# Toeplitz loads begun by SyncE alone, the first tile of a projection made ahead, and another order of pieces in the attention

## The chip, the cores and the metric

The kernel runs on one core of a Trainium2 chip. A core has five engines that each work through their own list of instructions in order: TensorE (PE, matrix multiplication, with its weight loads shown as PEld), VectorE (DVE), ScalarE (ACT), GpSimd (POOL) and SyncE (SP). Data moves between the chip's memory and the on-chip SBUF by DMA. A DMA is begun by an instruction on one of the engines (here SP, ACT or POOL), and that instruction stands in the engine's list like any other. Matrix products land in PSUM and are moved from there by DVE or ACT.

The metric is the device time of one execution in microseconds (us); the median of several runs is compared. A profile of one execution comes beside it.

## What is computed

The input is 8 images of 56 x 56 pixels with 192 channels, in float32. Four layers follow each other, each of the form x + f(group_norm(x)) with 32 groups. The first two are alike and take most of the time; cut to what matters:

```python
# layers 0 and 1, x normalized, 192 -> 576 channels
p = silu(x @ p_w.T + p_b)
q = silu(x @ q_w.T + q_b)
v = silu(x @ v_w.T + v_b)
qv = q * v
o1 = toeplitz(qv along w, a1)     # one 56-tap two-sided filter per channel
o2 = toeplitz(qv along h, a2)
out = (p * (o1 + o2)) @ o_w.T + o_b
```

Layer 2 is a 7 x 7 depthwise convolution, a layer norm and a two-layer MLP with GELU. Layer 3 is attention with 6 heads in shifted windows of 7 x 7:

```python
q, k, v = x @ Wq, x @ Wk, x @ Wv          # 6 heads of 32, windows of 49 tokens
attn = softmax(q @ k.T * sqrt(32) + bias + masks)
out = (attn @ v) @ Wfc + bfc
```

## The kernel before

**Layers 0 and 1.** The images are handled in two halves of four, named by j0 = 0 and 2. For each layer and half there are three parts, each a Python generator that yields now and then:

- `tno_qv` (Q): normalizes x, multiplies by the weights of q and v, applies Silu and the product, and stores qv to memory. It runs over groups of 256 tokens. A group's x comes by one DMA on SP (L222, buffer pool `t6`, three buffers) two groups ahead; it is normalized on ACT (`normalize`, L228, six instructions per group). A unit is up to 128 tokens by 512 columns: 16 matmuls for each 256 columns (L245), a bias addition on DVE (L254), Silu on ACT (L264), the product on DVE (L267) into a buffer of the pool `t4`, and a store by a DMA on SP (L270).
- `tno_toeplitz` (TZ): 9 blocks of 64 channels by two directions (d = 0 along w, d = 1 along h) make 18 steps; each layer and half has such a run, which makes 72 steps in all. A step n loads its matrices with two DMAs (`matrices`, L331, buffers `tm0` and `tm1` in turn) and its qv with two DMAs (L317, along w) or one (L320, along h) into one of two buffers `q`; both are asked for two steps ahead, when the last `along` of step n has been given out, because that frees the buffers. Then come eight `along` (32 matmuls, L343, and a copy to `ot` on ACT, L350) and eight `turned` (seven transposes on PE, L360, and a copy or an addition into `s` on DVE, L363 and L366). The sum is stored by POOL (L376).
- `tno_out` (O): for tiles of 224 tokens, loads x (L112, in a helper) and the sum s = o1 + o2 (L436) by DMAs on SP, normalizes x on DVE (`normalize`, three tensor_scalar, L442, into a `t4` buffer), multiplies by the gate's weights (L460, L475), takes Silu on ACT (L504, into two more `t4` buffers, and L521), multiplies s by the gate (L531), and multiplies that by the output weights for the tile before (L470, L492), adds x and stores.

`weave` runs a *lane*, a list of Q and O generators, and takes pieces of one Toeplitz generator in between, in proportion. When 90% of a generator's planned time is done it begins the next one (`then`) by calling it at each yield until it returns a value other than None. The lanes are: Q(0,0); Q(0,2) with TZ(0,0); O(0,0) and Q(1,0) with TZ(0,2); O(0,2) and Q(1,2) with TZ(1,0); O(1,0) with TZ(1,2); O(1,2) with layer 2. In the profile Q(0,2) lies from about 456 to 1090 us, the next three lanes end near 2080, 3150 and 3800 us.

**Layer 3** (`attention`). Sixteen units of half an image, each in three groups g of windows. In each group there are four slots, in which pieces of other units may be given to PE: after the scores of i = 0, after those of i = 1, after the transposes of the previous group's weights (`turned`, L1223), and between the two halves of the product with v (`weighted`, L1245). A table says which kind goes into each slot: 0 is the next unit's projection (`project`: Wq, Wk, Wv; 64 matmuls of L1155 in a piece, with copies L1168 on ACT and L1170 on DVE), 1 is the previous unit's output (`out`: matmuls L1271 in two pieces, drained from PSUM by DVE, L1282).

```python
order = ((0, 0, 0, 0), (0, 1, 1, 0), (0, 0, 0, 0))
```

**What sets the order.** The framework's scheduler decides each engine's order of instructions from a planned time of each; engines then run in order. PSUM is a pool of four buffers of two banks (`bank2`), so PE waits when the four before it have not been emptied.

Of the kernel before, what the change touches and what calls it, by code (L numbers as in the profile page):

```python
# [19 lines left out]
B, H, W, C = 8, 56, 56, 192  # L20
# [16 lines left out]
class Net:  # L37
# [266 lines left out]
    def tno_toeplitz(self, j0, tables, qv, o):  # L304

        nc, p = self.nc, self.tz
        PR = H // 2

        def load(n):
            blk, d = divmod(n, 2)
            q = p.tile([128, H, 128], F32, name="q", bufs=2)
            if d == 0:
                for half, eng in ((0, nc.sync), (1, nc.scalar)):
                    of = qv[2 * blk + half, :T].rearrange("(h w) e -> w h e", w=W)
                    eng.dma_start(q[64 * half : 64 * half + W], of)  # L317
            else:
                of = qv[2 * blk : 2 * blk + 2].rearrange("n (h w) e -> (n h) (w e)", w=W)
                nc.scalar.dma_start(q.rearrange("p i e -> p (i e)"), of)  # L320
            return q

        def matrices(n):

            blk, d = divmod(n, 2)
            tab = tables[d]
            for half in range(2):
                at = tab.offset + (blk * DC + 32 * half) * 112
                src = bass.AP(tab.tensor, at, [[1, H], [112, 32], [1, H]])
                to = self.tms[n % 2][64 * half : 64 * half + H, : 32 * H]  # L330
                nc.scalar.dma_start(to.rearrange("p (c w) -> p c w", w=H), src)  # L331

        def along(n, q, ot, g):


            tm = self.tms[n % 2]
            pt = self.bank2()
            for j in range(4):
                c = 4 * g + j
                for s in range(2):  # L340
                    for r in range(2):
                        rows = slice(64 * r, 64 * r + 56)
                        nc.tensor.matmul(  # L343
                            pt[64 * s : 64 * s + 64, r, j * 112 : (j + 1) * 112],
                            tm[rows, c * H : c * H + 64],
                            q[rows, PR * s : PR * s + PR, 4 * c : 4 * c + 4],
                            start=True,
                            stop=True,
                        )
            nc.scalar.copy(  # L350
                view(ot, 4 * g, [[112 * 32, 2], [32, 112], [1, 4]]),
                view(pt, 0, [[512, 2], [1, 112], [112, 4]]),
            )

        def turned(d, ot, s, r, i0, n):

            pz = self.bank2().rearrange("p k (i q) -> p (k i) q", q=128)
            for i in range(n):
                at = (r * PR + i0 + i) * 128
                nc.tensor.transpose(pz[:, i, :120], ot[:120, at : at + 128], self.ident[:120, :120])  # L360
            if d == 0:
                to = view(s, r * T + i0 * W + 55, [[W, n], [PR * W, 2], [-1, W]])
                nc.vector.tensor_copy(to, view(pz, 0, [[128, n], [64, 2], [1, 56]]))  # L363
            else:
                to = view(s, r * T + 55 * W + i0, [[-W, H], [PR, 2], [1, n]])
                nc.vector.tensor_add(to, to, view(pz, 0, [[1, 56], [64, 2], [128, n]]))  # L366

        def store(blk, s, half):
            for b in range(4):
                part, row = divmod(blk * DC + 32 * half, 128)  # L370
                if part < 4:
                    part += b // 2 * 4
                else:
                    part, row = 8, row + b // 2 * 64
                to = o[j0 + b % 2, part, row : row + 32, :]
                nc.gpsimd.dma_start(to, s[32 * b : 32 * b + 32, half, :])  # L376

        NS = 2 * (D1 // DC)
        loaded = []
        for n in range(2):  # L380
            loaded.append(load(n))
            matrices(n)
        yield 8.0

        late = []
        for n in range(NS):
            blk, d = divmod(n, 2)
            q = loaded.pop(0)
            ot = p.tile([128, 2 * PR * 128], F32, name="ot", bufs=1)
            if d == 0:  # L390
                s = p.tile([128, 2, T], F32, name="s", bufs=1)
            for g in range(8):
                along(n, q, ot, g)
                if g % 4 == 3:
                    if g == 7 and n + 2 < NS:
                        loaded.append(load(n + 2))
                        matrices(n + 2)
                    yield 3.2
                    for f in late:
                        store(*f)  # L400
                    late = []
            for u in range(8):
                turned(d, ot, s, u // 4, u % 4 * 7, 7)
                if u % 4 == 3:
                    yield 3.2
                    for f in late:
                        store(*f)
                    late = [(blk, s, u // 4)] if d == 1 else []
        for f in late:
            store(*f)  # L410

    def tno_out(self, L, j0, xs, gn, o, ys, gn_next):

        nc, p, inp = self.nc, self.tp, self.inp
        N = 224
# [16 lines left out]
        def load_s(j, t):  # L434
            s = p.tile([128, 9, N], F32, name="t8")
            nc.sync.dma_start(s, o[j, :, :, t * N : (t + 1) * N].rearrange("k p t -> p k t"))  # L436
            return s
# [104 lines left out]
        before = None  # L542
        x2 = load_x(*tiles[0])
        s = load_s(*tiles[0])
        yield 0.0
        xn = normalize(j0, x2[:, :, :N])
        done = None
        for n, (j, t) in enumerate(tiles):
            self.norm_part()
# [65 lines left out]
    def tno_layers(self, x0, x1, x2, gn, last):  # L615
# [3 lines left out]
        LS = ("L0", "L1")  # L619
# [9 lines left out]
        with ExitStack() as ctx, ExitStack() as wqp:  # L629
            self.wqp = wqp.enter_context(tc.tile_pool(name="wqp", bufs=1, side="right"))  # L630
            self.tp = ctx.enter_context(tc.tile_pool(name="tp", bufs=3))
            Q = lambda i, j0: self.tno_qv(LS[i], j0, x[i], gn[i], qvs[j0])
            O = lambda i, j0: self.tno_out(LS[i], j0, x[i], gn[i], o[i], x[i + 1], gn[i + 1])
            TZ = lambda i, j0: self.tno_toeplitz(j0, tables[i], qvs[j0], o[i])
            QT, OT, TZT = 25 * 2.25 * 5.3, 28 * 10.7, 8 + 72 * 3.2

            with tc.tile_pool(name="tab", bufs=2) as tab:
                self.input_stats(x0, gn[0], 0, tab)
                self.decay_tables("L0", tab, tables[0])
                first = Q(0, 0)  # L640
                for n in range(20):
                    next(first)
                self.input_stats(x0, gn[0], 2, tab)
                none = tab.tile([112, 512], F32, name="none", bufs=1)
                nc.gpsimd.memset(none, 0.0)
                for qv in qvs.values():
                    to = qv[:, T:].rearrange("n (p k) e -> p n (k e)", p=112)
                    nc.gpsimd.dma_start(to, view(none, 0, [[0, D1 // 32], [1, 512]]))
                self.decay_tables("L1", tab, tables[1])
                lanes = [[(first, QT)], [(Q(0, 2), QT)], [(O(0, 0), OT), (Q(1, 0), QT)]]  # L650
                lanes += [[(O(0, 2), OT), (Q(1, 2), QT)], [(O(1, 0), OT)], [(O(1, 2), OT)]]
                self.weave(lanes[0], after=lanes[1][0][0])
            with tc.tile_pool(name="tz", bufs=1) as self.tz:
                self.tms = []
                for i in range(2):
                    tm = self.tz.tile([120, 32 * H + 8], F32, name=f"tm{i}")
                    nc.gpsimd.memset(tm, 0.0)
                    self.tms.append(tm)
                for n, tz in enumerate((TZ(0, 0), TZ(0, 2), TZ(1, 0), TZ(1, 2))):
                    self.weave(lanes[n + 1], tz, lanes[n + 2][0][0], TZT)  # L660
                    if n == 2:
                        wqp.close()
            self.weave(lanes[5], **last())
# [320 lines left out]
    def attention(self, L, xs, gn3, gnd, ys, vd):  # L984
# [14 lines left out]
        if True:  # L999
# [321 lines left out]
            late = None  # L1321


            order = ((0, 0, 0, 0), (0, 1, 1, 0), (0, 0, 0, 0))
            for n in range(len(units) + 1):
                if n < len(units):
                    (b, hh), (v, qf, kf) = units[n], now
# [3 lines left out]
                for g in range(NG):  # L1331
# [1 line left out]
                        outs = out(*units[n - 1], *raws.pop(n - 1), oj)  # L1333

                    def give(at):
                        if order[g][at] and outs is not None:
                            step(outs)
                        elif not order[g][at] and gen is not None:
                            return step(gen)
                        return now  # L1340

                    es = []
                    for i in range(2):
# [218 lines left out]
```

## Time and profile before

| what | us |
|---|---|
| median of three runs | 6429.96 (6421.82 to 6434.29) |
| the profiled execution | 6428.51 |
| its span | 6426.7 (1.8 outside of it) |
| mean granted clock of TensorE | 0.943 |

By stretch, with PE's busy time, PE's clock (1.00 is full speed), the DMA engines' busy share and what they moved:

| stretch, us | work | PE busy | PEclk | DMA share | GB/s |
|---|---|---|---|---|---|
| 456 to 1090 | Q(0,2), TZ(0,0) | 558.06 | 0.93 | 0.84 | 223 |
| 1090 to 1650 | O(0,0), TZ(0,2) | 492.59 | 0.92 | 0.75 | 202 |
| 1650 to 2080 | Q(1,0), TZ(0,2) | 399.97 | 0.98 | 0.69 | 188 |
| 2080 to 2700 | O(0,2), TZ(1,0) | 552.58 | 0.92 | 0.71 | 196 |
| 2700 to 3150 | Q(1,2), TZ(1,0) | 413.03 | 0.96 | 0.66 | 181 |
| 3150 to 3800 | O(1,0), TZ(1,2) | 553.98 | 0.90 | 0.84 | 220 |
| 3800 to 4400 | O(1,2), layer 2 | 556.69 | 0.95 | 0.60 | 207 |
| 4400 to 5440 | layer 2 | 1022.88 | 0.99 | 0.37 | 117 |
| 5440 to 6427 | attention | 863.51 | 0.91 | 0.38 | 78 |

How to read lines of the profile: L343 is line 343 of the kernel. `out<-in` gives the buffers by their names in the program. A bracket at the end of a timeline line, as in `[2.85 <-DVE ra L1282]`, is the time for which the engine stood idle before, and what ended it. `ACTq` and `SPq` are the queues of DMA instructions on these engines: the length of such a line is the time in which the engine dealt with beginning the DMA, not that of the data's way. The page's last part lists DMAs by size:

```profile
q<-qv ACTq DMA_DIRECT2D x36, 3584.0 KB
...
tm<-L_tab ACTq DMA_DIRECT2D x144, 392.0 KB
q<-qv SPq DMA_DIRECT2D x36, 1568.0 KB
q<-qv ACTq DMA_DIRECT2D x36, 1568.0 KB
```

So the Toeplitz part begins its loads of q and of the matrices on both queues: 36 on SP and 36 + 36 + 144 on ACT.

### The profile page before, as it was taken

How to read it: one execution, taken by the hardware profiler on the slowest of the kernel's cores; microseconds unless marked ns; L12 is line 12 of the kernel's file. 1: busy time of each engine (PE TensorE's matmuls, PEld its weight loads, DVE VectorE, ACT ScalarE, POOL GpSimd, SP SyncE). 2: the span in 40 equal slices, each digit the busy share in tenths (PEclk: the TensorE clock that was granted, in tenths of full speed). 3: DMA queues.
4: the chain of work that ended last, by engine and by line, in shares of the span. 5: the costliest groups of instructions: out<-in, count | busy, mean ns of one | idle time of the engine just before them, and what ended most of it. 6: DMA issues, size and time to landing. Idle time of an engine off the chain costs nothing.

```text
span 6426.7 us, 151998 instructions
## 1 busy us (share of the span) xinstructions
PE 5783.7 (90%) x68832; PEld 4566.2 (71%) x68832; DVE 2860.1 (45%) x4858; ACT 2148.7 (33%) x2736; POOL 635.6 (10%) x829
## 2 busy tenths in 40 slices
PE   5998898899999899898888889998999999898897
PEld 3777787787777778777777778885666444666665
DVE  6554555344555444455434343324212322555555
ACT  2444343232444222344232323224323333333332
POOL 0000000000000000000000010000000100333332
PEclk9998999999999999999988999999999999999998
DMA  7448887777675677675698865664444322443432
GB/s 247 116 145 217 225 253 182 209 201 214 182 200 163 178 214 204 186 213 161 174 228 213 256 198 193 218 237 127 166 152 152 93 61 59 73 87 85 90 82 56
DMA packets 1240518, 1078.47 MB, mean 168 GB/s; under 512 B 452704, under 2 KB 1186912, under 8 KB 1224448
## 3 DMA queue, kind: packets, MB, share of 16 engines
q1 hardware_dynamic: 825768, 620.03, 34.9%
q10 hardware_dynamic: 378648, 247.74, 15.1%
q0 software_dynamic: 35456, 200.98, 9.8%
q8 instruction: 541, 8.86, 0.6%
q14 instruction: 105, 0.86, 0.0%
HBM read 712.50 MB, written 356.12 MB: 166 GB/s over the span
## 4 chain that ended last, share of the span: by engine, by line
PE 70%; DVE 10%; DMA 8%; ACT 5%; issue 3%; ACTq 2%; POOL 1%; SPq 1%; DVEq 0%; POOLq 0%
PE bank L245 16%; PE bank L360 7%; PE bank L881 6%; PE bank L460 5%; PE bank L470 5%; PE bank L343 5%; PE bank L742 5%; PE bank L961 4%; PE bank L1155 2%; PE bank L975 2%; DMA qv<-t 2%; PE bank L475 2%; PE bank L492 2%; ACT ot L350 2%; DVE t L254 2%
## 5 line engine op out<-in xcount | busy, mean ns | idle before, releaser
L245 PE MATMUL bank<-wq,t 64*128 64x256 f32 (+5 forms) x8000 | 1319.9, 372 | 66.9 <-ACT ot L350 49.1
L245 PEld LDWEIGHTS bank<-wq,t 64*128 64x128 f32 (+3 forms) x8000 | 1041.0, 189 | 319.1 <-issue 104.9
L264 ACT ACTIVATE t<-t 128x2048 f32<-128x2048 f32 (+1 forms) x300 | 439.9, 1482 | 960.8 <-DVE t L254 872.4
L254 DVE TENSOR_TENSOR t<-bank,wq 128x1024 f32<-128x1024 f32 (+2 forms) x500 | 540.2, 1113 | 477.1 <-PE bank L245 476.2
L360 PE MATMUL bank<-ident,ot 120*128 120x120 f32 x4032 | 549.0, 300 | 162.7 <-ACT ot L350 64.7
L360 PEld LDWEIGHTS bank<-ident,ot 120*128 120x128 f32 x4032 | 494.6, 160 | 222.7 <-DVE s L363 78.1
L504 ACT ACTIVATE t<-bank,wo 128x448 f32<-128x448 f32 x448 | 247.5, 635 | 1065.3 <-PE bank L475 795.8
L343 PE MATMUL bank<-q,tm 56*64 56x112 f32 x18432 | 522.6, 266 | 70.8 <-issue 32.8
L531 DVE TENSOR_TENSOR t<-t,t 128x896 f32<-128x896 f32 x224 | 241.4, 1090 | 752.9 <-ACT t L504 752.0
L343 PEld LDWEIGHTS bank<-q,tm 56*64 56x64 f32 x18432 | 482.1, 138 | 105.9 <-issue 57.1
L350 ACT COPY ot<-bank 128x896 f32<-128x896 f32 x576 | 481.6, 916 | 158.2 <-PE bank L343 157.4
L460 PE MATMUL bank<-t,wo 128*128 128x224 f32 x1792 | 405.1, 382 | 85.8 <-ACT t L504 46.4
L460 PEld LDWEIGHTS bank<-t,wo 128*128 128x128 f32 x1792 | 358.0, 207 | 106.5 <-ACT t L504 58.2
L267 DVE TENSOR_TENSOR t<-t 128x1024 f32<-128x1024 f32 (+1 forms) x300 | 280.5, 955 | 317.0 <-ACT t L264 253.8
L881 PE MATMUL bank<-z,w 128*128 128x448 f32 (+1 forms) x1344 | 413.2, 555 | 2.0 <-ACT h L890 2.0
L470 PE MATMUL bank<-t,wo 128*128 128x224 f32 x1792 | 367.2, 359 | 7.8 <-DVE t L531 4.9
L470 PEld LDWEIGHTS bank<-t,wo 128*128 128x128 f32 x1792 | 346.1, 194 | 11.9 <-DVE t L531 5.3
L363 DVE COPY s<-bank 128x784 f32<-128x784 f32 x288 | 267.7, 970 | 152.7 <-PE bank L360 122.9
L742 PEld LDWEIGHTS bank<-xt,cm 113*112 113x112 f32 x3072 | 309.2, 178 | 36.1 <-issue 31.7
L881 PEld LDWEIGHTS bank<-z,w 128*128 128x128 f32 (+1 forms) x1344 | 182.2, 189 | 205.5 <-issue 196.8
L376 POOL DMA_DIRECT2D L_sum<-s x288 | 141.0, 496 | 1821.5 <-DVE s L366 1816.0
L742 PE MATMUL bank<-xt,cm 113*112 113x108 f32 (+2 forms) x3072 | 317.4, 263 | 3.5 <-ACT h L890 2.4
(141 smaller groups left out, 6814.8 us busy)
## 6 DMA issues: line engine op xcount, KB each, us to landing
q<-qv ACTq DMA_DIRECT2D x36, 3584.0 KB
L_sum<-s POOLq DMA_DIRECT2D x288, 392.0 KB, 7.2
t<-L_sum SPq DMA_DIRECT2D x112, 1008.0 KB
qv<-t SPq DMA_DIRECT2D x192, 512.0 KB
cm<-in_L_cm SPq DMA_DIRECT2D x96, 896.0 KB
tm<-L_tab ACTq DMA_DIRECT2D x144, 392.0 KB
q<-qv SPq DMA_DIRECT2D x36, 1568.0 KB
q<-qv ACTq DMA_DIRECT2D x36, 1568.0 KB
```

The source lines that it names most:

```text
L245: nc.tensor.matmul(pp[:m, b, 256 * j : 256 * j + k], x[rows, j, 2 if part else b, s : s + m], w[rows, part, c0 + c : c0 + c + k],  start=p ...
L254: nc.vector.tensor_add(z[:m, c : c + k, :], view(pp[:m], 0, [[1, k], [256, 4]]), view(bias[:m], c0 + c, [[1, k], [0, 4]]),)
L264: nc.scalar.activation(z[:m, :n, :], z[:m, :n, :], AF.Silu)
L267: nc.vector.tensor_mul(prod[:m, :k], half[:, :, 0], half[:, :, 1])
L343: nc.tensor.matmul(pt[64 * s : 64 * s + 64, r, j * 112 : (j + 1) * 112], tm[rows, c * H : c * H + 64], q[rows, PR * s : PR * s + PR, 4 * c ...
L350: nc.scalar.copy(view(ot, 4 * g, [[112 * 32, 2], [32, 112], [1, 4]]), view(pt, 0, [[512, 2], [1, 112], [112, 4]]),)
L360: nc.tensor.transpose(pz[:, i, :120], ot[:120, at : at + 128], self.ident[:120, :120])
L363: nc.vector.tensor_copy(to, view(pz, 0, [[128, n], [64, 2], [1, 56]]))
L460: mm(gs[c // 2][:, b, c % 2 * 256 : c % 2 * 256 + N], pw[:, 0, 128 * c : 128 * c + 128], xn[:, b], start=c % 2 == 0, stop=False,)
L470: mm(P[:, b, :N], ow[:, c, 0:128], g[:, 4 * b + c], start=c == 0, stop=False)
L742: nc.tensor.matmul(pc[:, 128 * e + 4 * m0 : 128 * e + 4 * m1], cm[:113, e, k, :], xt[:, m0 - 1 + k : m1 - 1 + k, c + e, :], start=n == 0 a ...
L881: nc.tensor.matmul(phs[c][:, s, :TT], w0[rows, part, at : at + 128], z[rows, Z[2 if part else s], :], start=part == flip, stop=part != flip,)
```

## The change

It has three parts. First, the loads of q and of the matrices in `tno_toeplitz` are all begun by SP; before, ACT began one half of the pairs of L317 and all of L320 and L331. Second, `tno_out` takes a flag `early`: with it, the generator yields None after its first loads, so that `weave` calls it once more and the first tile's normalize is given out before the generator's own turn. It is set for all but O(1, 2). Third, the table of the attention's slots holds lists of kinds. In group 1 the second slot now takes an output piece and then a projection piece, the third slot an output piece, and the fourth none; before, the projection piece stood in the fourth.

```diff
-                for half, eng in ((0, nc.sync), (1, nc.scalar)):
+                for half in range(2):
                     of = qv[2 * blk + half, :T].rearrange("(h w) e -> w h e", w=W)
-                    eng.dma_start(q[64 * half : 64 * half + W], of)
+                    nc.sync.dma_start(q[64 * half : 64 * half + W], of)
             else:
...
-                nc.scalar.dma_start(q.rearrange("p i e -> p (i e)"), of)
+                nc.sync.dma_start(q.rearrange("p i e -> p (i e)"), of)
...
-                nc.scalar.dma_start(to.rearrange("p (c w) -> p c w", w=H), src)
+                nc.sync.dma_start(to.rearrange("p (c w) -> p c w", w=H), src)
...
-    def tno_out(self, L, j0, xs, gn, o, ys, gn_next):
+    def tno_out(self, L, j0, xs, gn, o, ys, gn_next, early):
...
         s = load_s(*tiles[0])
+        if early:
+            yield None
+            xn = normalize(j0, x2[:, :, :N])
         yield 0.0
-        xn = normalize(j0, x2[:, :, :N])
+        if not early:
+            xn = normalize(j0, x2[:, :, :N])
...
-            O = lambda i, j0: self.tno_out(LS[i], j0, x[i], gn[i], o[i], x[i + 1], gn[i + 1])
+            O = lambda i, j0, early=True: self.tno_out(LS[i], j0, x[i], gn[i], o[i], x[i + 1], gn[i + 1], early)
...
-                lanes += [[(O(0, 2), OT), (Q(1, 2), QT)], [(O(1, 0), OT)], [(O(1, 2), OT)]]
+                lanes += [[(O(0, 2), OT), (Q(1, 2), QT)], [(O(1, 0), OT)], [(O(1, 2, False), OT)]]
...
-            order = ((0, 0, 0, 0), (0, 1, 1, 0), (0, 0, 0, 0))
+            order = (((0,), (0,), (0,), (0,)), ((0,), (1, 0), (1,), ()), ((0,), (0,), (0,), (0,)))
...
-                        if order[g][at] and outs is not None:
-                            step(outs)
-                        elif not order[g][at] and gen is not None:
-                            return step(gen)
-                        return now
+                        got = now
+                        for kind in order[g][at]:
+                            if kind and outs is not None:
+                                step(outs)
+                            elif not kind and gen is not None:
+                                got = step(gen)
+                        return got
```

## The prediction

> **What bounds the kernel now.** I read the page's first and fourth part, then the waits of PE and of ACT, then busy times and clock by stretch, then the timeline around the largest stalls.
>
> ```profile
> PE 5783.7 (90%) x68832; PEld 4566.2 (71%) x68832; DVE 2860.1 (45%) x4858; ACT 2148.7 (33%) x2736; POOL 635.6 (10%) x829
> ...
> PE 70%; DVE 10%; DMA 8%; ACT 5%; issue 3%; ACTq 2%; POOL 1%; SPq 1%; DVEq 0%; POOLq 0%
> ```
> PE is the bound: it is idle for 6426.7 − 5783.7 = 643 us. The change adds and removes no PE work, so it can gain only from this idle time and from matmuls that run at half clock. The waits of PE that it touches (total us, times, longest):
>
> ```profile
> PE bank L360 <- ACT ot L350: 64.7, 27, 6.3
> PE bank L360 <- DVE s L363: 62.6, 53, 5.0
> PE bank L1271 <- DVE ra L1282: 47.0, 30, 3.6
> PE bank L460 <- ACT t L504: 46.4, 5, 17.5
> PE bank L460 <- DVE t L442: 32.6, 12, 8.1
> ```
> The second is untouched; it shows that not all waits of a Toeplitz step go. What ACT waits for shows who ends the fourth, and how late x tiles already come:
>
> ```profile
> ACT t L504 <- DMA qv<-t: 79.9, 3, 29.1
> ACT t L228 <- DMA t<-in_x: 66.1, 16, 13.9
> ```
> [...] In three consecutive stretches of an attention unit (PE, PEld, DVE, ACT, POOL busy, then PEclk, DMA share, GB/s) it falls after PE's idle and rises again:
>
> ```profile
> 5962.60:5971.90 9.30, 6.45 (x76) 4.26 (x72) 6.07 (x13) 2.48 (x4) 4.55 (x3) 1.00 0.44 69
> 5971.90:5978.70 6.80, 6.17 (x152) 4.58 (x152) 3.53 (x11) 0.00 (x0) 0.00 (x0) 0.50 0.34 120
> 5978.70:5985.50 6.80, 6.80 (x268) 5.07 (x264) 3.79 (x6) 2.25 (x2) 0.05 (x1) 1.00 0.62 163
> ```
> So a gap of 2.85 us costs up to 6.80 × 0.5 = 3.4 us more.
>
> [...] one L331 issue held ACT's queue for 16.6 us (longest of 144; median 0.34). [...]
>
> **Part 1, Toeplitz loads from ACT to SP.** 36 L317, 36 L320 and 144 L331 leave ACT (216 issues, 1295 to 1511 on SP). The recorded lengths of these issues add up to some 600 us of ACT's queue between 456 and 3800 us, but ACT is busy 33% and most of it lies beside idle ACT. What counts is what stands behind them. At a step's end an L331 waits until PE has read the old matrix, and the last copies L350 stand behind it:
>
> ```profile
> 1251.04 1.70 ACT L350 COPY ot<-bank 128x896 f32<-128x896 f32 x2
> 1252.40 0.31 ACTq L331 DMA_DIRECT2D tm<-L_tab  x1
> 1252.63 0.93 ACT L350 COPY ot<-bank 128x896 f32<-128x896 f32 x1
> 1252.78 1.97 ACTq L320 DMA_DIRECT2D q<-qv  x1
> 1253.42 0.94 ACT L350 COPY ot<-bank 128x896 f32<-128x896 f32 x1
> ```
> PE's L360 after it is idle 2.07 us, against about 1.1 where no issue stands between. There are 12 such ends of 2.0 to 2.1 us in the three lanes with tno_out: 12 × 0.9 = 11 us, and the six of the first two lanes are each followed by 3.4 us at half clock (1.7 us lost): up to 10, I take 8. In the lane from 456 to 1090 seven ends wait 3.2 to 6.3 us. In the new order of ACT's instructions the 2048-wide Silu L264 (1.9 us) stands ahead of the last copies there as now, so the five of 3.58 stay, and only 5.13 and 6.27 come down to that: 4 us. At each lane's start L320 (3.6 MB) is begun on ACT beside the qv stores, L267 waits for a store (11.1 us at 484), and PE for L254: 8.09 us at 479, and 3.80, 3.38 and 6.55 us in the two later stretches in which tno_qv runs beside the Toeplitz. In the new SP order this load comes 25 us later in the first lane: half of these 22, 10 us. The long issues leave little on PE (0.90 and 0.39 us after those of 15.3 and 16.6): 3. Sum 36, taken as **−35** (−15 to −60).
>
> Its price lies on SP. [...] from packet times in this trace (0.027 us for 512 B, 0.041 for 896 B) I estimate 14 to 16 us of full-rate transfer per step. Behind them stand L222 (next x of tno_qv), L270 (qv stores), L436 and L112 (s and x of tno_out). An SP issue that waits for its matrix or q buffer holds all of these. L222 has 7 to 19 us from issue to use where I followed it (611.5 to 625.6, 664.7 to 671.6, 721.8 to 729.7), L436 15 or more. Beside the times at which before issued them, the new order moves most neighbours by 1 to 5 us, and L222 behind stores by 8 to 11 in about 11 of 29 cases. With 28 x groups each 3 us later, ACT waits 84 us more in L228; of the 66 us it waits now in the lane from 456, PE shows about 19, so 84 × 19/66 = 24: **+25** (0 to +60).
>
> **Part 2, first tile of a projection ahead.** It acts where the last product of tno_qv meets the first tile of tno_out: 1110, 2117 and 3138 us (the fourth, O(1, 2), keeps the old way).
>
> ```profile
> 1111.01 0.32 ACTq L317 DMA_DIRECT2D q<-qv  x1
> 1111.43 1.91 ACT L264 ACTIVATE t<-t 64x2048 f32<-64x2048 f32 x1 [5.04 <-DMA q<-qv]
> ...
> 1142.99 2.21 ACT L504 ACTIVATE t<-bank,wo 128x448 f32<-128x448 f32 x4 [29.14 <-DMA qv<-t]
> ```
> These are ACT's; PE's, in the same place:
>
> ```profile
> 1115.38 6.30 PE L460 MATMUL bank<-t,wo 128*128 128x224 f32 x16 [5.44 <-DVE t L442]
> ...
> 1124.94 1.78 PE L460 MATMUL bank<-t,wo 128*128 128x224 f32 x8 [0.50 <-DVE t L442]
> ...
> 1144.20 3.35 PE L460 MATMUL bank<-t,wo 128*128 128x224 f32 x8 [17.48 <-ACT t L504]
> ```
> The L317 on ACT waits for stores to land and holds a Silu 5.0 us; with it L267 and then L442 are late, and PE loses 5.4. The last two stores go out at 1119 to 1122 behind the loads of q, x and weights and land at 1143; L504 waits for their t4 buffers, and PE loses 17.5. In the new order L442 stands about ten DVE instructions earlier, the L317 is on SP, and only its first half (1.6 MB, about 5.8 us) stands before the last two stores, which should land near 1120, about when PE has done the 10.5 us of gate matmuls it can do. Three times both (17.48 + 13.55 + 14.06, 3 × 5.4 and 3 × 0.5) are 62.8 us, and half clock over the matmuls that follow some 4 each: 75. Late next are the stores themselves (0 to 3 us) and the t4 buffer that the early tile holds during the last products (0 to 5): I take off 5 each. **−60** (−25 to −75). Three tensor_scalar and the loads of a tile move earlier and are none more; q(1), the L320 that now comes later, is first read some 90 us on.
>
> **Part 3, attention.** In 14 units the projection piece (64 matmuls, 1.54 + 0.96 us at L1155) moves from between the halves of L1245 to ahead of the transposes L1223. PE now finishes L1223 and waits 2.85 and then 0.63 us for PSUM that DVE empties:
>
> ```profile
> 5969.99 2.65 DVE L1282 SCALAR_TENSOR_TENSOR ra<-bank,bfc,ra 128x371 f32<-128x371 f32 x8
> ```
> The drains start where they did, after the row sum that waits for the exponentials. With the piece in front, 2.4 us of the gap are filled, but L1223 and the second L1271 then wait for the same buffers: 1.2 + 0.4 + 0.65 = 2.25 us against 3.5. So 1.25 × 14 = 17 us; if no gap is long enough to drop the clock, 14 × 3.4 = 48 more. With half of that, **−40** (0 to −65); below nothing only if L1245 then waits for L1233, now hidden by the second L1271 (4.8 us).
>
> **Sum.** −60 − 35 + 25 − 40 = −110: 6428.5 becomes 6318.5. The profiled run lies 1.5 us below the median of 6429.96, which gives 6320.
>
> **Rivals.** (1) *The cover of the DMA holds the gain* (DMA share is 0.84 in the lane from 456 and 0.84 from 3150). Late stores still end the three transitions, and the clock falls in attention anyway: −25 − 15 + 25 − 18 = −33, 6397. [...] Against: the stall of 17.5 us has one store order behind it, and that order changes. (2) *x tiles come late, slower*: in the three lanes with tno_qv beside the Toeplitz, L222 stands behind a whole step's block. The gains are 135 us; over 28 groups this decides at 4.8 us of PE time lost per group. At 6 it is 168 − 135 = +33, about 6463. For it: 66 us of such waits already, and slack as low as 7 us. Against: mostly 1 to 5 us of shift in the order. (3) *Part 3 does nothing*, its gap only moving: 6360. This lies in the forecast's own case.
>
> **How the numbers follow.** The forecast's case, 6260 to 6365, gets 0.62; rival 1 (to 6417) 0.20; no change 0.05; rival 2 0.13. A measurement here can tell about 0.2%, 13 us, from no change. Faster 0.82, same 0.05, slower 0.13. The range 6265 to 6415 leaves out rival 2, no change and the far end of the sum.
>
> **What would show it.** Right: L460's two waits fall from 46.4 + 32.6 to 25 or less (the fourth lane's stay); L360 on L350 from 64.7 to about 50; L1271 on L1282 falls with new small waits at L1223; PEclk rises in the transitions. Wrong: ACT's L228 waits for x well above 145 (66.1 + 78.9), PE idle behind them, SP issues of 10 us and more with L222 behind; attention as long as before; L504 still waiting 20 us for stores.

## The result and the profile after

The changed kernel takes 6267.16 us (median of four runs, 6264.8 to 6269.64) against 6427.83 us for the kernel before (median of four runs, 6421.82 to 6434.29): the ratio is 0.975, with a 95% interval of 0.9733 to 0.9767, or 160.7 us less. The forecast was 6320, 110 us less. The profiled span is 6263.0 us. Line numbers after L545 have moved by 4 and, from L1341 on, by 6: L1275 is the old L1271, L1286 the old L1282, L1227 the old L1223.

The first and fourth part of the page of the changed kernel:

```profile
PE 5694.4 (91%) x68832; PEld 4501.3 (72%) x68832; DVE 2853.2 (46%) x4858; ACT 2148.3 (34%) x2736; POOL 637.6 (10%) x829
...
PE 66%; DVE 10%; DMA 9%; ACT 6%; issue 5%; SPq 2%; POOL 1%; POOLq 0%; ACTq 0%; DVEq 0%
```

PE has done the same 68832 matmuls in 89.3 us less busy time (5783.7 − 5694.4), and the mean granted clock is 0.958 after 0.943 (at 0.50 for 525 us of the span, after 733 us): more of the matmuls ran at full clock. PE is idle 74 us less (643 to 568.6). What PE waited for, in the rows that answer to those of before (total us, times, longest):

```profile
PE bank L245 <- ACT ot L350: 100.5, 44, 11.2
...
PE bank L360 <- ACT ot L350: 56.4, 25, 5.5
...
PE bank L460 <- DVE t L442: 24.6, 5, 8.0
...
PE bank L1227 <- DVE ra L1286: 20.9, 14, 1.9
PE bank L1249 <- DVE et L1237: 18.4, 15, 2.1
...
PE bank L360 <- DVE s L363: 5.6, 2, 2.8
...
PE bank L1275 <- DVE ra L1286: 5.6, 14, 1.3
```

Three things are to be seen. The row that the prediction called untouched, L360 behind L363, is nearly gone: 62.6 to 5.6 us. L460 behind L504 (46.4) has gone altogether. And one row has doubled: L245 behind L350 is 100.5 us, and before it was

```profile
PE bank L245 <- ACT ot L350: 49.1, 37, 2.9
```

To see where the time went, the span is cut at the first matmul of each part (times from the traces, in us; the columns to the right are differences from before):

| stretch | before | after | loads alone (e1) | q alone (e4) | matrices alone (e10) | rotation (e9) |
|---|---|---|---|---|---|---|
| Q(0,2) with TZ(0,0) | 638.1 | +33.7 | +34.1 | +38.5 | +52.1 | +3.4 |
| O(0,0) with TZ(0,2) | 537.0 | −62.8 | −65.0 | −57.2 | −44.1 | −13.9 |
| Q(1,0) with TZ(0,2) | 470.2 | +10.0 | +16.2 | +30.1 | +34.0 | +11.2 |
| O(0,2) with TZ(1,0) | 543.7 | −70.1 | −73.6 | −63.0 | −49.2 | −25.2 |
| Q(1,2) with TZ(1,0) | 476.8 | +0.4 | +9.8 | +29.3 | +38.7 | +8.4 |
| O(1,0) with TZ(1,2) | 709.0 | −34.6 | −39.9 | −40.5 | −38.0 | −21.4 |
| attention from its first scores | 943.8 | −37.9 | +4.1 | −4.5 | −13.5 | −10.9 |

The rest of the span moves by 9 us or less. Each column is one execution, and stretches scatter: in e2 and e3 below, whose Toeplitz loads are those of before, a stretch of layers 0 and 1 differs from before by up to 13.3 us, and the attention takes 930 to 948 us with the old order in all these runs, 899 to 907 with the new one. The execution of e9 is its fastest, 24 us below its median. In these traces the gain is −167.5 in the three stretches with `tno_out` and −37.9 in the attention; +44.1 is given back where `tno_qv` runs beside the Toeplitz.

The same Toeplitz step shows most of it. PE before, at the step from 1207.5:

```profile
1207.55 0.94 PE L360 MATMUL bank<-ident,ot 120*128 120x120 f32 x7
1209.65 0.94 PE L360 MATMUL bank<-ident,ot 120*128 120x120 f32 x7 [1.17 <-DVE s L363]
1211.66 0.94 PE L360 MATMUL bank<-ident,ot 120*128 120x120 f32 x7 [1.07 <-DVE s L363]
1213.66 1.66 PE L360 MATMUL bank<-ident,ot 120*128 120x120 f32 x7 [1.07 <-DVE s L363]
1216.39 1.66 PE L360 MATMUL bank<-ident,ot 120*128 120x120 f32 x7 [1.07 <-DVE s L363]
1219.12 4.46 PE L360 MATMUL bank<-ident,ot 120*128 120x120 f32 x21 [1.07 <-DVE s L363]
```

and after, at the same step:

```profile
1222.64 5.96 PE L360 MATMUL bank<-ident,ot 120*128 120x120 f32 x56
```

Before, the eight groups of seven transposes run in turn with the copies of DVE, and from the fourth group on at half clock (1.66 instead of 0.94 us, PEclk 0.50 from 1213.7 to 1223.9): 1207.55 to 1223.4, or 15.8 us. After, all 56 run through in 6.0. The reason can be read from the two programs as built, in the PSUM buffers (named by their first bank) that these eight groups were given:

```
before: 2 2 2 2 2 2 4 2
after:  4 6 2 0 4 6 2 0
```

A buffer that holds the group just before is refilled only after DVE has emptied it: the five waits of 1.07 to 1.17 us above. Before, 72 of all 576 groups take their neighbour's buffer, in sixteen steps, all in stretches with `tno_out`; after, none does. PE's order of work is almost the same in both. The section on the kernel before was too simple here: PE does not wait until four earlier buffers are empty, but for the one buffer that the plan gave it, and the plan does not take the four in turn.

### The profile page after: what moved, and what is told of

It reads as the page before. It is cut to its first block, busy times and chain, and to the rows that moved or that the text cites. A ratio compares the mean times of both kernels' runs of the same rounds, so it can differ in the third digit from the quotient of the medians.

```text
span 6263.0 us, 151859 instructions
## 1 busy us (share of the span) xinstructions
PE 5694.4 (91%) x68832; PEld 4501.3 (72%) x68832; DVE 2853.2 (46%) x4858; ACT 2148.3 (34%) x2736; POOL 637.6 (10%) x829
## 3 DMA queue, kind: packets, MB, share of 16 engines
q1 hardware_dynamic: 1204416, 867.77, 53.7%
## 4 chain that ended last, share of the span: by engine, by line
PE 66%; DVE 10%; DMA 9%; ACT 6%; issue 5%; SPq 2%; POOL 1%; POOLq 0%; ACTq 0%; DVEq 0%
PE bank L245 15%; PE bank L360 6%; PE bank L885 6%; PE bank L746 5%; PE bank L460 5%; PE bank L470 5%; PE bank L965 4%; PE bank L343 4%; PE bank L979 2%; DVE t L254 2%; PE bank L475 2%; DMA t<-x 2%; ACT ot L350 2%; ACT t L264 2%; PE bank L492 2%
## 5 line engine op out<-in xcount | busy, mean ns | idle before, releaser
L245 PE MATMUL bank<-wq,t 64*128 64x256 f32 (+5 forms) x8000 | 1330.5, 374 | 115.8 <-ACT ot L350 100.5
L245 PEld LDWEIGHTS bank<-wq,t 64*128 64x128 f32 (+3 forms) x8000 | 1050.4, 191 | 369.0 <-ACT ot L350 111.3
L343 PE MATMUL bank<-q,tm 56*64 56x112 f32 x18432 | 533.9, 268 | 110.2 <-issue 54.5
L343 PEld LDWEIGHTS bank<-q,tm 56*64 56x64 f32 x18432 | 488.5, 139 | 150.3 <-issue 86.2
L360 PE MATMUL bank<-ident,ot 120*128 120x120 f32 x4032 | 482.7, 282 | 69.1 <-ACT ot L350 56.4
L504 ACT ACTIVATE t<-bank,wo 128x448 f32<-128x448 f32 x448 | 248.1, 636 | 832.4 <-PE bank L475 808.4
L350 ACT COPY ot<-bank 128x896 f32<-128x896 f32 x576 | 482.1, 915 | 138.8 <-PE bank L343 138.5
L360 PEld LDWEIGHTS bank<-ident,ot 120*128 120x128 f32 x4032 | 452.3, 150 | 107.7 <-ACT ot L350 62.1
L267 DVE TENSOR_TENSOR t<-t 128x1024 f32<-128x1024 f32 (+1 forms) x300 | 283.5, 956 | 387.5 <-ACT t L264 332.4
L460 PE MATMUL bank<-t,wo 128*128 128x224 f32 x1792 | 387.7, 371 | 25.2 <-DVE t L442 24.6
L460 PEld LDWEIGHTS bank<-t,wo 128*128 128x128 f32 x1792 | 346.0, 199 | 40.5 <-DVE t L442 16.8
L470 PE MATMUL bank<-t,wo 128*128 128x224 f32 x1792 | 362.7, 356 | 13.1 <-DVE t L531 10.7
L470 PEld LDWEIGHTS bank<-t,wo 128*128 128x128 f32 x1792 | 342.1, 192 | 16.0 <-DVE t L531 6.1
L363 DVE COPY s<-bank 128x784 f32<-128x784 f32 x288 | 260.4, 965 | 85.0 <-PE bank L360 45.1
```

The source lines that it names most:

```text
L245: nc.tensor.matmul(pp[:m, b, 256 * j : 256 * j + k], x[rows, j, 2 if part else b, s : s + m], w[rows, part, c0 + c : c0 + c + k],  start=p ...
L267: nc.vector.tensor_mul(prod[:m, :k], half[:, :, 0], half[:, :, 1])
L343: nc.tensor.matmul(pt[64 * s : 64 * s + 64, r, j * 112 : (j + 1) * 112], tm[rows, c * H : c * H + 64], q[rows, PR * s : PR * s + PR, 4 * c ...
L350: nc.scalar.copy(view(ot, 4 * g, [[112 * 32, 2], [32, 112], [1, 4]]), view(pt, 0, [[512, 2], [1, 112], [112, 4]]),)
L460: mm(gs[c // 2][:, b, c % 2 * 256 : c % 2 * 256 + N], pw[:, 0, 128 * c : 128 * c + 128], xn[:, b], start=c % 2 == 0, stop=False,)
L470: mm(P[:, b, :N], ow[:, c, 0:128], g[:, 4 * b + c], start=c == 0, stop=False)
```

## The experiments

After the result, and before the first of these runs, two theories stood against each other. A: the loads' part gains through those PSUM buffers. B, the prediction's: it gains because ACT's queue is no longer held by issues of DMAs. Ratios are against the kernel before, run beside each on the same chip.

**e1, the first part alone.** The three edits of `tno_toeplitz` and nothing else.

> The Toeplitz loads on SP alone, without the early tile and without the other order in attention. Theory A (PSUM buffers: in the program before, 72 of 576 groups of transposes L360 get the very PSUM buffer of the group just before them and so run in turn with DVE; with the loads off ACT none do): the 62.6 us of L360 behind L363 and most of the 24.9 behind L366 go, with some 30 us of half clock, and the later x tiles cost about 45: near 6350 us. Theory B (the prediction's: ACT's queue is held by the issues): -35 + 25, near 6418, and L360's waits for DVE stay above 50 us.

Measured: 6313.31 us, ratio 0.9806 (0.9778 to 0.9834), 119.0 us less than the 6432.3 beside it. L360's wait for L363 is 6.9 us. Theory A's sign and rows come true, and the gain is larger than its number: the three stretches with `tno_out` lose 178.5 us, which includes the transitions. Both marks of B are missed, 6418 us and waits for DVE above 50 us.

**e2, the second part alone.** The edits of `tno_out`, its flag and the lanes, as in the change.

> The early first tile alone. If the late L442 and the t4 buffers are the cause of the transitions' stalls (62.8 us): about -45, near 6385. If the loads' place on the queues causes them, as the order of the last two stores behind q loads suggests: less than -15, near 6415. L360's waits for DVE stay at 62.6 in both.

Measured: 6434.97 us, ratio 1.0005 (0.9993 to 1.0017), as the second of the two forecasts has it. The stall has only moved: PE's waits at the three transitions were 62.8 us before and are 75.0 here (28.02 + 23.47 + 23.53). PE of this run at the first transition, and under it the DVE instruction that it waits for:

```profile
1132.68 3.29 PE L460 MATMUL bank<-t,wo 128*128 128x224 f32 x16
...
1166.77 5.91 PE L460 MATMUL bank<-t,wo 128*128 128x224 f32 x16 [28.02 <-DVE t L442]
```

```profile
1166.22 1.01 DVE L442 TENSOR_SCALAR t<-t,gn 128x224 f32<-128x224 f32 x3 [26.56 <-DMA qv<-t]
```

The first tile's matmuls now start without a wait, but the second tile's normalize needs a `t4` buffer, and that is held by a qv store that has not landed. What was late were the stores; L442 and L504 only stood in line for them.

**e3, the third part alone.** The table of slots and the function `give` that reads it, as in the change.

> The attention's order alone. Prediction: -40, near 6388. The stretch from the first scores to the end was 943.8 us before and is 905.9 after: if the gain is the order's own, it is -38 here too; if it were owed to something earlier (DMA, weights), it would be under -20.

Measured: 6392.56 us, ratio 0.9939 (0.9919 to 0.9959), 39.7 us less. The attention's stretch is 900.1 us here, 43.7 shorter. The gain is the order's own.

**e4, only the q loads to SP.** The edits of L317 and L320; L331 stays on ACT.

> Only the loads of q (L317, L320) go to SP; the 144 matrix loads L331 stay on ACT with their waits and holds of up to 16 us. Theory A: 1 of 576 transposes' groups keeps its neighbour's buffer, so nearly the whole gain in the stretches with tno_out is there: within 25 us of e1. Theory B: the L331 ahead of the last copies still hold ACT, so half of e1's gain or more is missing.

Measured: 6364.82 us, ratio 0.9889 (0.9863 to 0.9914). This is 51.5 us above e1, more than the 25 that theory A allowed, and less than the half of e1's 119.0 us that theory B wanted missing. The table shows where they are. In the stretches with `tno_out` the gain is all but whole (−160.7 against −178.5), with 144 L331 still on ACT and L360's wait for L363 at 7.6 us. The difference lies in the stretches with `tno_qv` (+97.9 against +60.1). The total alone would have misled.

**e5, the buffers shared again in the changed kernel.** `turned` gets the tile of the group before it in the sixteen steps concerned.

```diff
-            pz = self.bank2().rearrange("p k (i q) -> p (k i) q", q=128)
+            if not same:
+                shared[0] = self.bank2()
+            pz = shared[0].rearrange("p k (i q) -> p (k i) q", q=128)
...
-                turned(d, ot, s, u // 4, u % 4 * 7, 7)
+                turned(d, ot, s, u // 4, u % 4 * 7, 7, 1 <= u <= one.get(n, 0))
```

> The changed kernel, but the groups of transposes that shared a PSUM buffer with their neighbour in the kernel before (72 of 576, in 16 steps of runs 1 to 3) are made to share it again; the loads stay on SP. Theory A: L360's waits for L363 and L366 come back to about 85 us, with some 30 us of half clock: 100 us or more above the changed kernel, near 6370. Theory B: the waits have another cause (ACT held by its DMA issues, and DVE behind it): under 30 us, below 6300.

Measured: 6292.84 us, ratio 0.9793 (0.9763 to 0.9822). The time lies where theory B put it, but it tests neither theory: the built program shows that the scheduler saw the sharing and put other matmuls between the groups, so none directly follows its neighbour in the same buffer any more, and the wait for DVE is 9.3 us. The state before could not be made again in this way.

**e6, the change without its second part.**

> The change without its early tile: loads on SP and the attention's order. e1 and e3 together gave -159 of the whole's -161. If the early tile is worth nothing: 6260 to 6280. If it has the -45 that the expectation of e2 gave it, beside the loads: 6310.

Measured: 6277.54 us, ratio 0.9769 (0.9741 to 0.9798), which overlaps the whole change's 0.9733 to 0.9767. The early tile is worth nothing that the times can tell, with the loads on SP (here) or without (e2). The traces do show a little beside the loads on SP: at the three transitions PE waits 23.0 us for L442 in this run, and 15.6 in the whole change.

**e7 and e8, x of `tno_qv` begun by another engine.** `nc.sync` of L222 becomes `nc.scalar` (e7) or `nc.gpsimd` (e8) in the changed kernel.

> The changed kernel with the x loads of tno_qv (L222) begun by ACT. If these loads are late [...], their ACT waits (209 us) fall below 80 and the three stretches with tno_qv get back most of their +44: near 6230. If DMA as a whole is the limit there: within 10 us of 6267. A loss would show as ACT holding its own copies behind a waiting x load.

> The same loads begun by POOL, which is busy 10%: as e7, near 6230, but without holding ACT; POOL's stores L376 would stand behind a waiting x load, which costs little since they have slack.

Measured: e7 6329.24 us, ratio 0.9845 (0.9818 to 0.9872); e8 6243.59 us, ratio 0.9718 (0.9688 to 0.9748). In neither do ACT's waits for x fall: they are 305 us in e7 and 232 in e8, against 209 in the changed kernel and 145 before. With x begun by ACT these waits are 96 us longer than in the changed kernel, and the kernel loses. On POOL it is 34 us faster than e6 (6277.54), which ran on the same chip but lacks the early tile; against the whole change (0.9733 to 0.9767) the intervals overlap. The stretches with `tno_qv` give back 28.7 us where the change gives 44.1, but 39.2 in e11, which begins the loads in the same way, so it is not shown where the gain lies. It does not come from the waits that were to fall below 80: x that no longer stands on SP's queue is not earlier.

**e9, the kernel before with a fixed rotation of PSUM.** All loads are where they were.

```diff
-        ps = ctx.enter_context(tc.tile_pool(name="ps", bufs=4, space=PSUM))
-        self.bank2 = lambda: ps.tile([128, 2, 512], F32, name="bank2")
+        ps = ctx.enter_context(tc.tile_pool(name="ps", bufs=1, space=PSUM))
+        self.turn = 0
+
+        def bank2():
+            self.turn = (self.turn + 1) % 4
+            return ps.tile([128, 2, 512], F32, name=f"bank2{'abcd'[self.turn]}")
+
+        self.bank2 = bank2
```

> The kernel before, all its loads where they were (ACT and SP), but its four PSUM buffers are handed out in a fixed rotation instead of by planned time; 12 instead of 72 of the 576 groups of transposes then take their neighbour's buffer. Theory A: L360's waits for L363 and L366 fall from 87 to below 30 us, and the time by 50 to 100: 6330 to 6380. Theory B (ACT held by its issues): within 20 us of before, and L360's waits for DVE above 50.

Measured: 6408.45 us, ratio 0.9966 (0.9953 to 0.9979): 22 us less, not half of the least that A expected, and just beyond B's 20. Lines are 6 higher here: L366 is the transposes, L369 and L372 what DVE does with them, L510 the gate's Silu on ACT, L337 the loads of the matrices. What ended PE's waits at the transposes (us, times):

```profile
  ACT ot L356: 63.1, 27
  ACT t L510: 60.9, 9
  DVE s L369: 22.0, 15
  DVE s L372: 10.9, 10
```

The waits for DVE are down from 87.5 (62.6 behind L363 and 24.9 behind L366 before) to 32.9 us, a little more than A said and less than B's 50. In their place stand 60.9 us behind Silus of the gate, which are late on ACT and hold PSUM; before, this wait was 1.5 us. The trace shows why they are late. One of the nine, first on ACT and then on PE:

```profile
1289.86 15.01 ACTq L337 DMA_DIRECT2D tm<-L_tab  x1
1304.97 1.16 ACT L510 ACTIVATE t<-bank2b,wo 128x448 f32<-128x448 f32 x2 [18.90 <-issue]
```

```profile
1306.18 1.66 PE L366 MATMUL bank2b<-ident,ot 120*128 120x120 f32 x7 [10.09 <-ACT t L510]
```

In all nine, ACT's queue is held by an issue of a matrix load for 13.9 to 16.8 us, and the Silu begins 0.1 us after its end. So when the plan gave the transposes one buffer, the others really were held. Theory A names the wait, B what lies behind it, though the instructions held are the gate's Silus and not the copies L350 that the prediction named. With the loads where they were, a wait at this place is paid in one form or the other: in the three stretches with `tno_out` PE's idle time is 227.3 us here and was 226.5 before, and only its busy time fell, from 1563.2 to 1502.0, with fewer matmuls at half clock. With either part of the loads taken off ACT (e4 and e10), both forms of the wait are all but gone: 9.2 and 11.4 us for DVE, 2.7 and none for L504.

**e10, only the matrices to SP.** The edit of L331 alone.

> Only the matrix loads L331 go to SP, the loads of q keep both queues; 1 group of transposes keeps its neighbour's buffer. Theory A: the stretches with tno_out as short as in e4, -57, -63, -40. For the price in the stretches with tno_qv: [...] it is here about half of e1's +34 and +16 in the first two; if it comes from the issues of L331 waiting on SP in front of x and stores, it is all here.

Measured: 6405.65 us, ratio 0.9958 (0.9936 to 0.998). One group of transposes shares its neighbour's buffer, L360 waits 9.4 us for L363, and the stretches with `tno_out` gain 131.3 us: 75.1 of PE's busy time and 56.1 of its idle time. The transitions are as before: L460 still waits for L504,

```profile
PE bank L460 <- ACT t L504: 47.4, 3, 18.4
```

so it is the move of the q loads (e4) that ends them, not that of the matrices. The price in the stretches with `tno_qv` is +124.8, more than with all loads on SP, so neither of the two forecasts of it holds. The trace shows one difference: in these stretches the issues of L331 took 304 us of SP's time here and 199 in the changed kernel.

**e11, e8 with the fixed rotation of e9.**

> The changed kernel with x by POOL (e8) and PSUM in a fixed rotation (e9). No reuse by neighbours is left to remove, so the rotation can only move waits: within 25 us of e8, near 6245; slower if the plan's choice of the earliest free buffer was worth something elsewhere.

Measured: 6242.31 us, ratio 0.9697 (0.9675 to 0.9719): not to be told from e8, and as expected. e8 and e11 are the fastest that were run, and the interval of e11 lies clear of the change's.

**e12, the matrices begun by POOL in the changed kernel.** `nc.sync` of L331 becomes `nc.gpsimd`.

> The changed kernel with the matrix loads L331 begun by POOL; q, x and qv stay on SP. e10 put only L331 on SP and lengthened the three stretches with tno_qv by 52, 34 and 39 us, more than all the loads together (34, 10, 0). If it is L331 in front of x and stores on SP's queue that costs there: the three come down to below +15 in all, near 6235. [...] +40 stays, near 6265. If POOL takes long over these loads of many short rows, steps wait for matrices (L343 behind L331) and it is slower than the changed kernel.

Measured: 6435.75 us, ratio 0.9996 (0.9982 to 1.001). The three stretches with `tno_qv` are +91.0, +38.2 and +30.2; ACT waits 340 us for x. The price is higher than the first two forecasts have it. The third has the slower time right but not its reason: no step's first matmul (L343) waits for its matrices. Taking L331 from in front of x on SP does not lower the price. That L331 costs nothing there is not shown, since the loads may cost in another way when POOL begins them.

## Why the prediction was right, and where it was not

The sign was right, and the measured 6267 lies in the range of 6265 to 6415, 2 us from its end. The gain was half as large again as forecast. The sum came out through terms of which one was right, one too small, one put to the wrong part, and one missing, so that it came this near is in part luck: for the loads alone −10 was forecast (−35 + 25) and −119.0 measured, for the early tile −60 and nothing that the times can tell. Of its signs of being right, the two waits of L460 fell to 24.6 us (25 were said); of its signs of being wrong, ACT's waits for x came too, 209 us.

**Part 3, −40: right in size and in its two terms.** Alone it measures −39.7. The attention's stretch before and after (length, then PE's busy time, further on PEclk):

```profile
5483.00:6426.70 943.70, 821.65 (x22104) 627.91 (x22104) 533.45 (x860) 312.30 (x377) 294.24 (x210) 0.91 0.38 79
```

```profile
5357.20:6263.00 905.80, 799.28 (x22104) 607.01 (x22104) 530.55 (x860) 309.32 (x377) 295.08 (x210) 0.94 0.39 83
```

PE's idle time fell from 122.1 to 106.5, or 15.5 us (17 were said), and its busy time by 22.4 for the same matmuls (24 were said for the half clock). The new waits are where they were put: L1227 for DVE 20.9 us, and also L1249 for L1237, 10.3 before (L1245 for L1233) and 18.4 now, which the prediction named as the way to lose.

**Part 2, −60: the stalls went, but not through this part.** The sum of the three transitions was read correctly and most of it is gone. The step that failed is "with it L267 and then L442 are late", from which an earlier L442 was to be part of the cure: with the L317 off ACT and no early tile (e1), the first L442 still costs PE 4.02 us at each transition, against 5.4 before. e2 and e6 give the early tile no time that can be told from nothing. The cure is the other clause of the same step, the order in which the last qv stores and the q loads are begun, and it belongs to part 1: the waits behind L504 are gone in e1 and e4 and still there in e10. In the changed kernel PE still loses a second tile's normalize at each of the three:

```profile
1146.66 3.29 PE L460 MATMUL bank<-t,wo 128*128 128x224 f32 x16
1157.93 5.42 PE L460 MATMUL bank<-t,wo 128*128 128x224 f32 x16 [5.21 <-DVE t L442]
```

**Part 1, −35 at the steps: the argued term hardly came, and the large one was called untouched.** The prediction counted the L331 ahead of the last copies, and L360 behind L350 went only from 64.7 to 56.4 us: 8.3, not the 15 of its idle terms at the ends of steps (11 + 4). In the three stretches with `tno_out`, where the 11 were to come, it went from 31.5 to 30.2: ten of the twelve ends still wait 2.0 to 2.2 us with no issue on ACT, so the issue was not what made them long. (In the lane from 456 there are eight ends of 3.2 to 6.3 us, not seven; this does not change the sum.) What the prediction left out is the row just under that one in the same view. "The second is untouched" was the failing sentence: L360 behind L363 was taken as a trait of the transposes, although seven other steps of the same kernel ran their 56 in 6.0 to 6.1 us. e10, with the transitions unchanged, measures −131.3 in these stretches, and its waits for DVE at the transposes are 76 us shorter. The profile shows that PE waits for DVE there; that a PSUM buffer had been handed out again at once shows only in the built program.

**Part 1, +25 for SP: the right place, too small, and its cause only in part shown.** The stretches with `tno_qv` cost +44.1, and 39.2 to 64.4 in the four traces with all of these loads on SP (the change, e1, e5, e6). ACT's waits for x rose from 145.1 to 209.2 (84 more were said, 64 came); they are 145 to 178 in the four traces with the loads as before (before, e2, e3, e9) and 197 to 212 in those four. One of them, first on SP, then on ACT and then on PE, in the changed kernel:

```profile
785.14 8.99 SPq L317 DMA_DIRECT2D q<-qv  x2
794.19 9.88 SPq L331 DMA_DIRECT2D tm<-L_tab  x1
804.18 7.16 SPq L222 DMA_DIRECT2D t<-in_x  x1
```

```profile
815.91 2.56 ACT L228 ACTIVATE t<-t,gn 128x256 f32<-128x256 f32 x5 [10.57 <-DMA t<-in_x]
```

```profile
821.12 3.23 PE L245 MATMUL bank<-wq,t 128*128 128x128 f32 x16 [7.34 <-ACT ot L350]
```

SP needs 19 us to begin one step's loads before it comes to x, ACT stands 10.57 us, and the next copies L350 stand behind the normalize on ACT, so PE loses 7.34 us: this is the row that doubled. From the traces, SP's time in issues over the three stretches rose from 222 to 735 us. That x's place on SP is the whole cause is not shown: without x on SP (e8) ACT waits for it 232 us. It also stays open why the loads cost more when a part of them is begun elsewhere: +124.8 with q on both queues, +97.9 with q on SP alone and the matrices on ACT, +159.4 with the matrices on POOL, against +44.1 with all of them on SP. Rival 2 thus had the right place, far from its point of decision (44.1 us are 1.6 per group, not 4.8); rival 1 fell with the transitions, whose 17.5 us did hang on one order of stores.

**The transitions and the sum.** The gains of part 1 are −178.5 + 60.1 in the cut spans of e1, and part 3 has −39.7; 119.0 + 39.7 = 158.7 of the 160.7 measured, so the parts add up without the early tile.

## What to carry to other kernels

When a matrix engine's groups wait one by one for the engine that empties them, look at which PSUM buffers they were given before calling it a limit of that engine: here the planner gave 72 of 576 groups the buffer of the group before. Then look at what holds the other buffers: here it was an engine's own DMA issues, up to 16.8 us long, with the instructions that empty PSUM behind them. A stall at a hand-over between stages is worth following to the last DMA that has not landed; here, preparing the next stage early only moved the wait to its second tile (62.8 us at the three before, 75.0 in e2). A change of queues is judged by stretches, since the same edit can gain in one stage and lose in the next (−178.5 and +60.1 us in e1).

## What the runs showed that was not expected

Beginning a part of the loads on another engine again did not make x earlier. ACT's waits for x are 209 us with all loads on SP, 280 with the matrices on SP and q on both queues (e10), and 340 with the matrices on POOL (e12), whose issues are 1.1 us each; that run fell back to the time of the kernel before. Yet the kernel before, with the matrices and most of q on ACT, has the least, 145.

The prediction has no term for packets that take longer. The DMA engines' packets of SP's and ACT's queues (q1 and q10) took more time on one queue than on two: 34.9% + 15.1% of 16 engines over 6426.7 us before and 53.7% over 6263.0 us after, for the same 1.2 million packets, which is 4.7% more. With a part of the loads moved it is between, 1.7% more in e10 and 3.5% in e4. Before, and then after:

```profile
q1 hardware_dynamic: 825768, 620.03, 34.9%
q10 hardware_dynamic: 378648, 247.74, 15.1%
```

```profile
q1 hardware_dynamic: 1204416, 867.77, 53.7%
```

The clock fell without a long gap. In the step at 1207.55 of the kernel before, PE stood idle for 1.17, 1.07 and 1.07 us, with 0.94 us of work between, and the next 10 us ran at half clock (length, PE's busy time, further on PEclk):

```profile
1207.50:1213.70 6.20, 2.90 (x24) 2.18 (x22) 4.76 (x8) 2.54 (x5) 0.76 (x1) 1.00 1.06 240
1213.70:1223.90 10.20, 8.06 (x37) 7.24 (x38) 5.01 (x8) 0.00 (x0) 0.00 (x0) 0.50 1.10 234
```
